# Normalisations and node scalings of a four-layer graph network: element work moved from VectorE to ScalarE, and one addition made by TensorE

## The chip, the cores and the metric

The kernel runs on one core of a Trainium2 chip. A core has five engines that run side by side, each with its own in-order queue of instructions: TensorE (PE in the profile; PEld is its loading of weights), VectorE (DVE), ScalarE (ACT), GpSimd (POOL) and SyncE (SP, which here only issues DMAs). They wait for one another through semaphores. The metric is device time in microseconds (us) from start to end of one execution; the median of three runs before the change is 2919.82 us.

## The reference

16 graphs (B) of 1024 nodes (N) with 64 features (H), each with a dense 1024 x 1024 fp32 adjacency. Four layers follow one another, and each begins with the same normalisation:

```
def _layernorm(x, axis=-1, eps=1e-5):
    m = jnp.mean(x, axis=axis, keepdims=True)
    v = jnp.var(x, axis=axis, keepdims=True)
    return (x - m) / jnp.sqrt(v + eps)
...
h = jnp.maximum(_layernorm(x, axis=-1), 0.0)
x = x + layer(h, adj)
```

- Layer 0: two small dense layers with relu, a product with the adjacency, and a gated (GRU) update.
- Layer 1: with `d = rowsum(adj + I) ** -0.5`, `relu(d_i * sum_j (adj + I)_ij * d_j * (h @ kernel)_j)`.
- Layer 2: part of the neighbours is struck off; per node and feature a weighted sum of three interpolated quantiles over the neighbours that are left (`agg`); then `relu((h + agg) @ W1 + b1) @ W2 + b2`, times the node mask.
- Layer 3: `(adj + I) @ h` divided by the row sums of `adj + I`.

## The kernel before

A tile holds the 1024 nodes of a graph as 128 partitions x 8 groups (`NT = 8`) x 64 features, so `X` and every feature tile of that kind is 128 x 512 fp32. A per-node number is a 128 x 8 tile; `over_h` broadcasts it over the 64 features.

The work on one graph is split into stages, each a Python generator: `load` (TensorE transposes the adjacency, ScalarE copies the result into `strip` and makes signs `sgn` of it), `code`, `rank`, `list` (which neighbours each node keeps, mostly VectorE), `mid` (`dense01`, lines 1277 to 1372: layers 0 and 1 and the normalisation of layer 2), `gath` (GpSimd fetches rows of neighbours' features, the table `tab`, with indirect DMAs), `sort` (VectorE sorts them with min/max networks; tiles `hb`, `s`, `o`), `sums` (ScalarE weights the sorted values, VectorE adds them), and `rear` (`dense23`, lines 1647 to 1699: rest of layer 2, and layer 3).

The order of all instructions is fixed before the program runs, by the planner `Order` (lines 191 to 273). It simulates the engines with costs from `Engine.duration` (326 to 356) and always takes a step of the stage that can start first; on a tie, the stage that is earlier in a list: `rear`, `sums` and `gath` come first, then `mid`, `list`, `rank` and `code`, then `load` and `fetch`, and `sort` last (1784). A generator's `yield "A", x` says that its next step is on ScalarE and needs `x`. The planner prices:

```
if self.letter == "V": ... return (cols + 74) / 960 + ..., 0.08
if self.letter == "A":
    return 0.09 + cols / 1130 + (0.2 if len(outs) > 1 else 0.0), 0.1
```

So changed steps change the order of everything around them. Stages of up to five graphs (`DEPTH = 5`) are under way at once. All instructions are issued by the helper at line 387, which is why the profile shows that line everywhere and tiles have to be told apart by name.

What the change touches: `layernorm_relu` (1181 to 1201), called three times in `dense01` (1281, 1344, 1370) and once in `dense23` (1683), 64 times over the 16 graphs; in `dense01` the product of the normalised `h` by `dinv` into `tr` (1353) and the update of X with `u1` (1362 to 1366); in `dense23` the addition of `agg` (gathered into `zz`) and `h2` with the transposition that follows (1661 to 1664), the product of the second dense layer's result by the node mask `nm` (1675 to 1679), and the division by the row sums (1688 to 1697). `transposed` (1206) and `back` (1216) are transpositions by TensorE; a `bank` is a PSUM buffer, given back by `close`. The tag `t2m` (and `t2r` in `dense23`) names two buffers that `t2` tiles share in turn; `hm` and `hr`, the normalised features, have one buffer each. In the profile tile names lose their trailing digits: `u1` and `u3` are `u`, `y2` is `y`.

The profile's line numbers are those of this listing.

Of the kernel before, what the change touches and what calls it, by code (L numbers as in the profile page):

```python
# [9 lines left out]
F32 = mybir.dt.float32  # L10
# [4 lines left out]
AF = mybir.ActivationFunctionType  # L15
ALU = mybir.AluOpType
AX = mybir.AxisListType

P = 128
# [373 lines left out]
def kernel(  # L393
# [29 lines left out]
    B, N, H = x.shape  # L423
    NT = N // P
    G = 3 * H
    HQ = q_W1.shape[1]
    NH = N // 512
# [4 lines left out]
    ident = const.tile([P, P], F32, name="ident")  # L432
# [75 lines left out]
    def over_h(v):  # L508
        return v[:, :, None].to_broadcast([P, NT, H])

    def lists_for_all():
        order = Order()
        V, A, T = Engine(nc.vector, "V", order), Engine(nc.scalar, "A", order), Engine(nc.tensor, "T", order)
# [10 lines left out]
        def bank(dtype=F32):  # L524
            return ps1.take([P, 512 * 4 // mybir.dt.size(dtype)], dtype, "bank")
# [42 lines left out]
        for k in range(8):  # L568
            v = NBITS * 2.0**k
# [608 lines left out]
                )  # L1178
                base += nr // 2 * q

        def layernorm_relu(X, h=None, who="m"):
            yield "V", X
            s = wp.tile([P, NT], F32, name="ln_s", bufs=2)
            V.reduce_sum(s, X, AX.X)
            V.tensor_scalar(s, s, -1.0 / H, None, ALU.mult)
            xc = wp.tile([P, NT, H], F32, name="ln_xc", tag="t2" + who, bufs=2)
            V.tensor_add(xc, X, over_h(s))
            sq = wp.tile([P, NT, H], F32, name="ln_sq", tag="t2" + who, bufs=2)
            yield "A", xc
            A.activation(sq, xc, AF.Square)  # L1190
            yield "V", sq
            v = wp.tile([P, NT], F32, name="ln_v", bufs=2)
            V.reduce_sum(v, sq, AX.X)
            yield "A", v
            A.activation(v, v, AF.Sqrt, bias=eps, scale=1.0 / H)
            yield "V", v
            V.reciprocal(v, v)
            if h is None:
                h = wp.tile([P, NT, H], F32, name="h" + who, bufs=1)
            V.scalar_tensor_tensor(h, xc, 0.0, over_h(v), ALU.max, ALU.mult)  # L1200
            return h

        def t2(name, who="m"):
            return wp.tile([P, NT, H], F32, name=name, tag="t2" + who, bufs=2)

        def transposed(h, dst):
            for i in range(NH):
                yield "T", h
                pt = yield from bank()
                for t in range(4):  # L1210
                    T.transpose(pt[0:H, t * P : (t + 1) * P], h[:, 4 * i + t, :], ident)
                yield "A", pt
                A.copy(dst[:, i * 512 : (i + 1) * 512], pt[0:H, :])
                ps1.close(pt)
# [62 lines left out]
        def dense01(b, S):  # L1277
            X = wp.tile([P, NT, H], F32, name="X", bufs=2)
            S_.dma_start(X, x[b].rearrange("(t p) h -> p t h", p=P))

            h = yield from layernorm_relu(X)
            cat = wp.tile([P, N], F32, name="cat")
            yield from transposed(h, cat[0:H, :])
            yield "T", cat
            m1T = wp.tile([P, N], F32, name="m1T", tag="big")
            pm = yield from product(w1, cat[0:H])
            yield from evicted(pm, m1T[0:H], AF.Relu, b1)
            yield "T", m1T
            p2 = yield from bank()
            T.matmul(p2, *bias(0), start=True, stop=False)  # L1290
            ams = streamed(b, 0)
            for t in range(NT):
                o = p2[:, t * H : (t + 1) * H]
                T.matmul(o, m1T[0:H, t * P : (t + 1) * P], w2, start=False, stop=t == NT - 1)
            yield "A", p2
            A.activation(m2x[:, :, 0:H], p2.rearrange("p (t h) -> p t h", h=H), AF.Relu)
            ps1.close(p2)
            pm = yield from propagated(b, m2x, 0, ams)

            yield "A", pm  # L1300
            A.copy(m1T[H : H + 1, :], pm[H : H + 1, :])
            yield from evicted(pm, cat[H:P], AF.Relu)
            yield "T", m1T
            pr = yield from bank()
            for t in range(NT):
                T.transpose(
                    pr[:, t : t + 1], m1T[H : H + 1, t * P : (t + 1) * P], ident[H : H + 1, H : H + 1]
                )
            yield "V", pr
            S["rs"] = rs = st.tile([P, NT], F32, name="rs")  # L1310
            V.tensor_scalar(rs, pr[:, 0:NT], 1.0, None, ALU.add)
            ps1.close(pr)
            rz = wp.tile([P, NT, 2 * H], F32, name="rz", tag="big")
            nn = t2("nn")
            for g in range(2):
                yield "T", cat
                pg = yield from bank2()
                for i in range(4):
                    t = 4 * g + i
                    o = pg[:, i * 4 * H : (i + 1) * 4 * H]  # L1320
                    if i % 2 == 0:
                        T.matmul(pg[:, i * 4 * H : (i + 2) * 4 * H], *bias(2), start=True, stop=False)
                    T.matmul(o, cat[:, t * P : (t + 1) * P], wg, start=False, stop=i % 2 == 1)
                pgv = pg.rearrange("p (i c) -> p i c", c=4 * H)
                gs = slice(4 * g, 4 * g + 4)
                yield "A", pg
                A.activation(rz[:, gs, :], pgv[:, :, 0 : 2 * H], AF.Sigmoid)
                yield "V", rz
                V.tensor_mul(nn[:, gs, :], pgv[:, :, 2 * H : G], rz[:, gs, 0:H])
                V.tensor_add(nn[:, gs, :], nn[:, gs, :], pgv[:, :, G : 4 * H])  # L1330
                ps2.close(pg)
            yield "A", nn
            A.activation(nn, nn, AF.Tanh)
            yield "V", nn

            d0 = t2("d0")
            V.tensor_sub(d0, h, nn)
            V.tensor_mul(d0, d0, rz[:, :, H : 2 * H])
            V.tensor_add(d0, d0, nn)
            V.tensor_add(X, X, d0)  # L1340

            ams = streamed(b, 1)

            h = yield from layernorm_relu(X)
            dinv = wp.tile([P, NT], F32, name="dinv", bufs=2)
            V.tensor_scalar(dinv, rs, 1e-30, None, ALU.max)
            yield "A", dinv
            A.activation(dinv, dinv, AF.Sqrt)
            yield "V", dinv
            V.reciprocal(dinv, dinv)  # L1350
            V.scalar_tensor_tensor(dinv, rs, 0.0, dinv, ALU.is_gt, ALU.mult)
            tr = t2("tr")
            V.tensor_mul(tr, h, over_h(dinv))
            pm = yield from propagated(b, tr, 1, ams, own=True)
            g0 = wp.tile([P, N], F32, name="g0", tag="big")
            yield from evicted(pm, g0[0:H])
            yield "T", g0
            pm = yield from product(wk, g0[0:H])
            g1 = wp.tile([P, N], F32, name="g1", tag="big")
            yield from evicted(pm, g1[0:H])  # L1360
            pa = yield from back(g1[0:H])
            yield "V", pa
            u1 = t2("u1")
            V.tensor_mul(u1, pa, over_h(dinv))
            ps1.close(pa)
            V.scalar_tensor_tensor(X, u1, 0.0, X, ALU.max, ALU.add)

            yield "S", X
            S_.dma_start(D[b % DEPTH]["x1"].rearrange("(t p) h -> p t h", p=P), X)
            h2 = yield from layernorm_relu(X)  # L1370
            yield "S", h2
            S_.dma_start(D[b % DEPTH]["tab"][1 : N + 1, :].rearrange("(t p) h -> p t h", p=P), h2)
# [274 lines left out]
        def dense23(b, S):  # L1647
# [7 lines left out]
            for t in range(NT):  # L1655
# [2 lines left out]
                    out=zz[:, t, :], out_offset=None, in_=d["agg"][:, :],  # L1658
                    in_offset=bass.IndirectOffsetOnAxis(ap=S["posi"][:, t : t + 1], axis=0),
                )  # L1660
            yield "V", zz
            V.tensor_add(zz, zz, h2)
            zT = wp.tile([P, N], F32, name="zT", tag="big3")
            yield from transposed(zz, zT[0:H])
            yield "T", zT
            uT = wp.tile([P, N], F32, name="uT", tag="big3")
            pm = yield from product(v1, zT[0:H])
# [4 lines left out]
            for t in range(NT):  # L1672
                o = py[:, t * H : (t + 1) * H]
                T.matmul(o, uT[:, t * P : (t + 1) * P], v2, start=False, stop=t == NT - 1)
            yield "V", py
            y2 = t2("y2", "r")
            V.tensor_mul(y2, py.rearrange("p (t h) -> p t h", h=H), over_h(nm))
            ps1.close(py)
            V.tensor_add(X, X, y2)

            ams = streamed(b, 3)
# [3 lines left out]
            g3 = wp.tile([P, N], F32, name="g3", tag="big3")  # L1685
            yield from evicted(pm, g3[0:H])
            pa = yield from back(g3[0:H])
            yield "V", pa
            u3 = t2("u3", "r")
            rd = wp.tile([P, NT], F32, name="rd", bufs=2)  # L1690

            V.scalar_tensor_tensor(rd, rs, 0.0, rs, ALU.is_equal, ALU.add)
            V.reciprocal(rd, rd)
            V.tensor_mul(u3, pa, over_h(rd))
            ps1.close(pa)
            res = t2("res", "r")
            V.tensor_add(res, X, u3)
            yield "S", res
# [472 lines left out]
```

## Time and profile before

| | |
|---|---|
| median of 3 runs (range) | 2919.82 us (2914.99 to 2942.51) |
| the profiled execution, its own time | 2917.36 us |
| its span (first to last instruction) | 2915.5 us, 31549 instructions |
| mean granted TensorE clock | 0.732 |
| VectorE busy, instructions | 2520.7 us (86%), 6678 |
| ScalarE busy, instructions | 1260.2 us (43%), 3138 |
| GpSimd busy, instructions | 1782.6 us (61%), 1598 |
| TensorE matmul busy | 1852.8 us (64%) |
| DMA | 427.11 MB, 146 GB/s over the span |

The page of the profile gives busy times, 40 equal slices with the busy share of each engine in tenths, and groups of instructions: engine, operation, output <- inputs, partitions x elements and type, times; then busy us, mean ns of one, and the engine's idle time just before them with what ended it. A row of the waits view reads: engine, tile, `<-` what it waited for, then us in total, times, longest. A row of the chain reads: start in us, duration, what ran. A share of busy time is a mean over stages with different limits; the stretches and the waits say which holds where.

### The profile page before, as it was taken

What the parts mean: (1) busy time and instruction counts of PE and PEld (TensorE: products, weight loads), DVE (VectorE), ACT (ScalarE), POOL (GpSimd) and SP (SyncE); (2) the same over time, 40 slices, a digit from 0 to 9 for tenths busy, and PEclk for the clock granted to TensorE, in tenths of its full rate; (3) what the DMA queues carried; (4) which work ended last, traced back from release to release, by engine and by line L of the source; (5) the groups of instructions that cost most, each with busy time, mean ns of one, the idle gap of its engine ahead of it and who ended that gap; (6) DMA issues with size and microseconds to landing.
All of it is one profiled execution on the core that took longest, in us unless ns stands there. A gap on an engine that the chain in (4) does not pass through costs nothing. (4 is left out here: it accounts for less than half of the span.)

```text
span 2915.5 us, 31549 instructions
## 1 busy us (share of the span) xinstructions
PE 1852.8 (64%) x8258; PEld 937.5 (32%) x8258; DVE 2520.7 (86%) x6678; ACT 1260.2 (43%) x3138; POOL 1782.6 (61%) x1598
## 2 busy tenths in 40 slices
PE   5876768677577776656856766767665865442223
PEld 3443333334233333233332433334232422121111
DVE  3659899988989979999798988899899799989792
ACT  7666373436445445335254355344445343030201
POOL 3047673746847567575656747566674667677761
PEclk6977779778787776877867667767876877656566
DMA  6667565465565546455564556536565643222222
GB/s 187 198 201 211 146 180 182 128 196 156 181 173 154 182 133 193 122 160 154 147 172 112 161 142 189 155 107 184 148 176 138 175 132 105 59 63 62 62 60 76
DMA packets 395166, 427.11 MB, mean 146 GB/s; under 512 B 165980, under 2 KB 302754, under 8 KB 394978
## 3 DMA queue, kind: packets, MB, share of 16 engines
q1 hardware_dynamic: 344386, 374.35, 41.9%
q0 software_dynamic: 50592, 50.66, 9.4%
q8 instruction: 68, 1.11, 0.2%
q14 instruction: 120, 0.98, 0.1%
HBM read 340.38 MB, written 84.46 MB: 146 GB/s over the span
## 5 line engine op out<-in xcount | busy, mean ns | idle before, releaser
L387 POOL DMA_INDIRECT s<-tab,idxL x864 | 1036.7, 1200 | 263.3 <-issue 259.1
L387 POOL DMA_INDIRECT gh<-tab,idxH x544 | 577.6, 1062 | 722.8 <-DVE idxH L387 169.6
L387 DVE TENSOR_TENSOR hb<-hb 128x128 f32<-128x128 f32 (+11 forms) x1072 | 739.1, 725 | 32.0 <-ACT hb L387 26.8
L387 PE MATMUL bank<-am,hr 128*64 128x512 f32 x512 | 281.9, 699 | 128.3 <-DVE hr L387 80.5
L387 PE MATMUL bank<-am,tr 128*64 128x512 f32 x512 | 270.4, 664 | 101.0 <-DVE tr L387 79.6
L387 PE MATMUL bank<-am,m2x 128*65 128x512 f32 x512 | 265.5, 662 | 45.1 <-DMA am<-adjT 40.5
L387 DVE TENSOR_TENSOR hb<-hb,hb 128x656 f32<-128x656 f32 (+2 forms) x256 | 252.3, 1000 | 3.9
L387 PE MATMUL bank<-ident,a 128*128 128x128 f32 x1024 | 202.3, 353 | 46.2 <-DMA a<-in_adj_dram 23.9
L387 ACT ACTIVATE s<-s,wl 128x64 f32<-128x64 f32 x704 | 180.3, 341 | 78.2 <-DVE s L387 78.2
L387 ACT COPY strip<-bank 128x512 f32<-128x512 f32 x256 | 143.5, 585 | 132.9 <-PE bank L387 121.1
L387 POOL DMA_INDIRECT zz<-agg,posi x128 | 141.4, 1104 | 87.4 <-DMA agg<-s 41.3
L387 PE MATMUL bank<-ident,gh 128*128 128x128 f32 x272 | 89.0, 352 | 154.1 <-DMA gh<-tab,idxH 153.3
L387 PEld LDWEIGHTS bank<-ident,a 128*128 128x128 f32 x1024 | 156.4, 183 | 77.5 <-issue 23.4
L387 PE MATMUL bank<-cx,oh 128*128 128x133 f16 (+1 forms) x1280 | 157.1, 279 | 35.5 <-DVE oh L387 25.4
L387 PEld LDWEIGHTS bank<-am,hr 128*64 128x64 f32 x512 | 74.6, 159 | 307.0 <-issue 137.1
L387 ACT ACTIVATE sgn<-strip 128x1024 bf16<-128x1024 f32 x128 | 135.2, 1056 | 53.0 <-PE bank L387 39.5
L387 ACT ACTIVATE junk<-bank,nkey 128x1024 bf16<-128x1024 f32 x128 | 140.7, 1108 | 27.5 <-PE bank L387 27.4
L387 PEld LDWEIGHTS bank<-am,tr 128*64 128x64 f32 x512 | 68.4, 150 | 237.6 <-issue 145.3
L387 ACT ACTIVATE g<-bank 64x512 f32<-64x512 f32 x96 | 52.0, 584 | 213.3 <-PE bank L387 213.3
L387 DVE TENSOR_TENSOR s<-s,o 128x576 f32<-128x576 f32 (+5 forms) x256 | 139.2, 552 | 2.8
L387 DVE TENSOR_TENSOR o<-s 128x1152 f32<-128x1152 f32 (+2 forms) x192 | 140.0, 754 | 1.6 <-DMA gh<-tab,idxH 0.2
L387 PE MATMUL bank<-w,sgn 128*128 128x32 bf16 x1024 | 49.8, 184 | 142.8 <-DVE sgn L387 97.2
(340 smaller groups left out, 3634.0 us busy)
## 6 DMA issues: line engine op xcount, KB each, us to landing
am<-adjT SPq DMA_DIRECT2D x384, 512.0 KB
a<-in_adj_dram SPq DMA_DIRECT2D x128, 512.0 KB
adjT<-strip SPq DMA_DIRECT2D x128, 512.0 KB
s<-tab,idxL POOLq DMA_INDIRECT x864
gh<-tab,idxH POOLq DMA_INDIRECT x544
wb<-wd SPq DMA_DIRECT2D x32, 198.0 KB
X<-in_x_dram SPq DMA_DIRECT2D x16, 256.0 KB
x<-X SPq DMA_DIRECT2D x16, 256.0 KB
```

The lines of the kernel that those rows point to most:

```text
L387: return f(*args, **kw)
```

## The change

- `layernorm_relu`: the centred copy `xc` and the tile of squares are gone. ScalarE takes the squares straight from X, one instruction for each of the 8 groups, with minus the mean as bias and the sum over the features from the instruction's accumulator; the squares themselves are written into the place of the result and overwritten later. VectorE multiplies minus the mean by the reciprocal deviation, and ScalarE makes `relu(X * v - mean * v)`, again 8 instructions. A new argument `times` multiplies the reciprocal deviation by a further per-node number.
- Layer 1's `tr` comes out of the normalisation so, with `times = dinv`; `dinv` is made ahead of it.
- A new helper `scaled` multiplies by a per-node number on ScalarE, 8 instructions; it takes the place of VectorE's product in `u1` (with the relu), `y2` and `u3`.
- The addition of `h2` to `zz` is made by TensorE: the transposition of `zz` becomes a product with the identity, and a second product adds `h2`.

```diff
-        def layernorm_relu(X, h=None, who="m"):
+        def layernorm_relu(X, h=None, who="m", times=None):
             yield "V", X
             s = wp.tile([P, NT], F32, name="ln_s", bufs=2)
             V.reduce_sum(s, X, AX.X)
             V.tensor_scalar(s, s, -1.0 / H, None, ALU.mult)
-            xc = wp.tile([P, NT, H], F32, name="ln_xc", tag="t2" + who, bufs=2)
-            V.tensor_add(xc, X, over_h(s))
-            sq = wp.tile([P, NT, H], F32, name="ln_sq", tag="t2" + who, bufs=2)
-            yield "A", xc
-            A.activation(sq, xc, AF.Square)
-            yield "V", sq
+            yield "A", s
             v = wp.tile([P, NT], F32, name="ln_v", bufs=2)
-            V.reduce_sum(v, sq, AX.X)
-            yield "A", v
+            if h is None:
+                h = wp.tile([P, NT, H], F32, name="h" + who, bufs=1)
+            for t in range(NT):
+                A.activation(h[:, t, :], X[:, t, :], AF.Square, bias=s[:, t : t + 1], accum_out=v[:, t : t + 1])
             A.activation(v, v, AF.Sqrt, bias=eps, scale=1.0 / H)
             yield "V", v
             V.reciprocal(v, v)
-            if h is None:
-                h = wp.tile([P, NT, H], F32, name="h" + who, bufs=1)
-            V.scalar_tensor_tensor(h, xc, 0.0, over_h(v), ALU.max, ALU.mult)
+            if times is not None:
+                V.tensor_mul(v, v, times)
+            V.tensor_mul(s, s, v)
+            yield "A", s, v
+            for t in range(NT):
+                A.activation(h[:, t, :], X[:, t, :], AF.Relu, bias=s[:, t : t + 1], scale=v[:, t : t + 1])
             return h
+
+        def scaled(dst, src, by, func=AF.Copy):
+            for t in range(NT):
+                A.activation(dst[:, t, :], src[:, t, :], func, scale=by[:, t : t + 1])
...
-            h = yield from layernorm_relu(X)
             dinv = wp.tile([P, NT], F32, name="dinv", bufs=2)
...
             V.scalar_tensor_tensor(dinv, rs, 0.0, dinv, ALU.is_gt, ALU.mult)
-            tr = t2("tr")
-            V.tensor_mul(tr, h, over_h(dinv))
+            tr = yield from layernorm_relu(X, t2("tr"), "m", dinv)
...
-            yield "V", pa
+            yield "A", pa
             u1 = t2("u1")
-            V.tensor_mul(u1, pa, over_h(dinv))
+            scaled(u1, pa, dinv, AF.Relu)
             ps1.close(pa)
-            V.scalar_tensor_tensor(X, u1, 0.0, X, ALU.max, ALU.add)
+            yield "V", u1
+            V.tensor_add(X, X, u1)
...
-            yield "V", zz
-            V.tensor_add(zz, zz, h2)
             zT = wp.tile([P, N], F32, name="zT", tag="big3")
-            yield from transposed(zz, zT[0:H])
+            for i in range(NH):
+                yield "T", zz, h2
+                pt = yield from bank()
+                for t in range(4):
+                    o = pt[0:H, t * P : (t + 1) * P]
+                    T.matmul(o, zz[:, 4 * i + t, :], ident, start=True, stop=False)
+                    T.matmul(o, h2[:, 4 * i + t, :], ident, start=False, stop=True)
+                yield "A", pt
+                A.copy(zT[0:H, i * 512 : (i + 1) * 512], pt[0:H, :])
+                ps1.close(pt)
...
-            yield "V", py
+            yield "A", py
             y2 = t2("y2", "r")
-            V.tensor_mul(y2, py.rearrange("p (t h) -> p t h", h=H), over_h(nm))
+            scaled(y2, py.rearrange("p (t h) -> p t h", h=H), nm)
             ps1.close(py)
+            yield "V", y2
             V.tensor_add(X, X, y2)
...
-            yield "V", pa
+            yield "V", rs
             u3 = t2("u3", "r")
             rd = wp.tile([P, NT], F32, name="rd", bufs=2)
             V.scalar_tensor_tensor(rd, rs, 0.0, rs, ALU.is_equal, ALU.add)
             V.reciprocal(rd, rd)
-            V.tensor_mul(u3, pa, over_h(rd))
+            yield "A", pa, rd
+            scaled(u3, pa, rd)
             ps1.close(pa)
+            yield "V", u3
             res = t2("res", "r")
             V.tensor_add(res, X, u3)
```

## The prediction, made before the changed kernel ran

> **What bounds the kernel now.** I read the page first (busy shares and the 40 slices), then the busy times in stretches of 100 us, the groups with their shapes kept apart, the waits, the chain that ended last, and single stretches of the timelines.
>
> ```profile
> PE 1852.8 (64%) x8258; PEld 937.5 (32%) x8258; DVE 2520.7 (86%) x6678; ACT 1260.2 (43%) x3138; POOL 1782.6 (61%) x1598
> ...
> DVE  3659899988989979999798988899899799989792
> ```
>
> VectorE (DVE) is the fullest engine (second line: tenths busy in 40 slices), and outside the fill (the first 200 us) and the tail (the last 65 us) it is at 79 to 97% in every stretch. ScalarE (ACT) is at 67 to 72% in the first 300 us, at 40 to 53% until 2400, then at 11 to 29%. From 200 to 2800 us VectorE stands idle for only 238 us of 2600 (the stretches of 100 us, summed), and what ends those gaps is spread thin:
>
> ```profile
> DVE oc L387 <- PE bank L387: 32.5, 11, 10.9
> DVE idxH L387 <- PE bank L387: 29.6, 10, 6.8
> DVE sgn L387 <- ACT sgn L387: 29.6, 13, 4.0
> DVE hb L387 <- ACT hb L387: 26.8, 7, 11.9
> ```
>
> These are its four longest (us in total, times, longest). Adding up this view over all rows, ScalarE ends 145 us of VectorE's waits and TensorE 138 us. So the bound is VectorE's own work plus small gaps; the sorting stages, which come last in the planner's order of stages, fill VectorE whenever nothing else is ready. The tail is different: there the chain is a latency chain through one graph. Its normalisation reads:
>
> ```profile
> 2882.31 0.70 DVE ln_s L387
> 2883.03 0.18 DVE ln_s L387
> 2883.24 0.70 DVE ln_xc L387
> 2883.96 0.64 ACT ln_sq L387
> 2884.62 0.70 DVE ln_v L387
> 2885.35 0.31 ACT ln_v L387
> 2885.68 0.21 DVE ln_v L387
> 2885.91 0.70 DVE hr L387
> ```
>
> From the first sum to `hr` ready: 4.3 us, of which VectorE is busy 3.2 us.
>
> **What the Trainium skill says.** "Perfetto Trace Analysis", section Identifying the Most-Contended Engine, takes the engine of highest occupancy as the one to relieve; here that is VectorE at 86%, so work taken from it should count. "VectorE: DVE Perf Modes", section on the TRN2 errata, gives an fp32 two-tensor operation (N+151)/0.96 ns, an estimate of 691 ns at N = 512; the trace has 692. "ScalarE: Activation LUTs", section What ACT_TABLE_LOAD costs, gives an ACTIVATE 186 ns + 0.833 ns per element, 93 ns more for each per-partition scale or bias, and 93 ns of overlap between neighbours. For 64 columns and one such operand that is an estimate of 239 ns from start to start; the trace has 15 of `s<-s,wl` (64 columns, a per-partition scale) in 3.69 us, so 0.246. Its section Rules for kernel authors sends relu and mul to VectorE; this change goes against that, and per operation it does lose (below).
>
> **The change part by part.** Rows, from the groups with shapes kept apart:
>
> ```profile
> L387 DVE TENSOR_REDUCE ln_v<-ln_sq 128x8 f32<-128x512 f32 x64 | 43.2, 675 | 4.5 <-ACT ln_sq L387 4.2 <-issue 0.2
> ...
> L387 DVE TENSOR_TENSOR ln_xc<-X,ln_s 128x512 f32<-128x512 f32 x48 | 33.4, 697 | 1.6
> ...
> L387 DVE SCALAR_TENSOR_TENSOR hm<-ln_xc,ln_v 128x512 f32<-128x512 f32 x48 | 33.3, 693 | 1.7
> ...
> L387 ACT ACTIVATE s<-s,wl 128x64 f32<-128x64 f32 x704 | 180.3, 341 | 78.2 <-DVE s L387 78.2
> ...
> L387 ACT ACTIVATION_READ_ACCUMULATOR junk<-bank,nkey 128x1 f32 x128 | 25.7, 201 | 0.0
> ```
>
> VectorE, removed. The first three rows with the `Xr` and `hr` forms of the last two (11.1 each) are 64 normalisations times three operations: 44.5 + 43.2 + 44.4 = 132 us. One large product or sum in each of five places a graph goes too: `tr` 11.1, `u<-bank,dinv` 10.9, `zz` 11.0, `y` 10.9, `u<-bank,rd` 11.1: 55 us. (The update of X with `u1` only changes its form.) Together 187. Added: a 128x8 product `s*v` in each normalisation and a product by `dinv` in 16 of them: 80 small operations at 0.19 (the reciprocal's row, 12.4/64): 15 us. Net 172. Neighbours on VectorE overlap: on its timeline a 0.69 us operation gives way to an independent one after 0.60 to 0.61, so 272 large operations may be worth 22 us less: 150. I take 160, and 15/16 of it, 150, as lying in the stretch that VectorE bounds; graph 0's normalisations lie in the fill, graph 15's last part in the tail.
>
> ScalarE, added. Squares: 8 a normalisation, each with a per-partition bias and an accumulator. No row has exactly that. The accumulator's read lasts 201 ns, but on the timeline a `junk` pair needs only 0.09 more than its ACTIVATE, as the read overlaps. Bounds: 0.25 (free) to 0.45 (read not overlapped); I take 0.246 + 0.09 = 0.34, so 2.7 us. Relus: 8 with scale and bias; one more operand is 0.09 by the skill's price, so 0.34 (0.25 to 0.43), 2.7 us. The old Square over 512 columns, 0.63, goes. +4.8 us in 64 normalisations = 306 us. The scalings `u1`, `y2`, `u3`: 48 times 8 times 0.246 = 94 us. ScalarE rises by 400 us to about 1660, 57% of the span (+310 at the lower, +500 at the upper prices). Table loads stay at 34: Square, Relu and Copy cause none now, and the order sigmoid, tanh, square root stays.
>
> TensorE. A transposition of `zz` (8 in 1.92 us in the tail) becomes 16 fp32 products with the identity; 8 such, `ident,hr`, take 1.91. So +1.9 us a graph, 30 in all, on an engine at 64%, hidden under VectorE's sort (30 us if TensorE were the bound).
>
> Buffers. `ln_xc` and `ln_sq` leave the two `t2` buffers, so those waits can only shrink. `hm` is written earlier, at the squares, and must wait for the previous graph's store to `tab`; that store is issued ahead of the next X load on the same SP queue, so I cost it nothing (if not covered: 2.6 us, the longest that a first sum waited for its X load, would be 42 over 16 graphs). No DMA is added or moved past another.
>
> Chains. A normalisation becomes 0.70 + 0.18 + 2.75 + 0.31 + 0.21 + 0.19 + 2.75 and hops, 7.2 us: 2.9 later than the 4.3 above. `tr` gains 0.69 back and loses a product: +2.4. `u1`, `y2`, `u3` take 2.0 for 0.70: +1.3 each. Fill (graph 0, before its first gather): 2.9 + 2.4 + 1.3 + 2.9 = 9.5. Tail: 2.9 + 1.3 + 1.3 + 1.9 (products) - 0.7 (no `zz` addition) = 6.7. Together 16 us. Elsewhere the chain is longer by the same 16 us a graph, hidden by the sort: X is loaded every 154 us (first 42.0, last 2349.8) and graph 0's middle stage took 107.
>
> New waits. ScalarE's queue is in order. Behind a block of 8 squares or relus stand the evictions of `strip`, `keys`, `cx` and `rz`, on which VectorE's `sgn`, `keys` and `nn` steps wait. I let the 145 us that ScalarE ends grow with its load, 400/1260 = 32%: 47 us, and the 138 of TensorE, which waits for banks to be emptied, by a tenth: 14. The planner prices a 64-column ACTIVATE at 0.09 + 64/1130 = 0.15 us against 0.25 here, so it sets VectorE's three additions up to 0.8 us too early: 38 us if all of it is felt, I take a third, 12. Sum 73, bounds 0 and about 230.
>
> Sum: 2915.5 - 150 + 16 + 73 = 2854 us of span. The profiled execution lies 2.4 us under the median of the runs and 1.9 over its span, so a median of about **2859 us**, 2.1% less.
>
> **Rivals.**
> (a) ScalarE's queue becomes the pace-setter, slower than before. For it: half of VectorE's gaps already end in ScalarE, it is at 70% in the fill, and it loses on every operation moved: 5.4 us for the 0.63 + 2.06 that it replaces. Against: at 57% it has 1250 us to spare, and its own idle is mostly waiting for VectorE and TensorE. It decides from where the gaps grow by 134 us (283 by 47%); at a growth of two thirds, 190, the span is 2915 - 150 + 16 + 190 = 2971.
> (b) Another engine takes over, and about half of the gain goes. GpSimd's gathers are 1782.6 busy and 424 of issue (259.1 + 124.0 + 40.7), 2206 in all, and from 2600 to 2800 us it shows 79% busy, which with 0.3 of issue per gather is full. If the gathers of the last two graphs set the end, what VectorE saves there is lost: 2915 - 75 + 16 + 40 = 2896, no change. Against: in the waits view VectorE waits 24 us for gathers, 14 of them in the tail.
> (c) Nearly no new waits, as the planner orders around them: 2915 - 150 + 16 = 2781. This is the forecast's mechanism with its smallest price.
>
> **How the numbers follow.** Forecast, gaps growing by 30 to 120 us (2811 to 2901): 0.48. (c): 0.14. (b): 0.16. (a): 0.22. About 1% is what a measurement of this kernel can tell from no change; that is 2891 and 2949. Of the forecast 0.45 is below 2891 and, with (c) and a little of (b), faster is 0.63. (a) from 2949 on gives slower 0.19; the rest, 0.18, is the same. The range reaches from (c) with the higher removal (172 for 160: 2770) to the beginning of (a), 2960.
>
> **What would show it.** Right: `ln_xc` and `ln_sq` gone; VectorE near 2350 to 2370 busy, ScalarE near 1660; 512 accumulator reads more; squares 0.34 and relus 0.34 from start to start; VectorE's waits on ScalarE near 200. Wrong: VectorE below 82% busy in the middle stretches, with waits on `h`, `keys`, `nn`, `u` or `sgn` grown past 280; or the same 90% with GpSimd at 79% throughout.

## The result and the profile after

| | before | after |
|---|---|---|
| median (18 runs each, range) | 2923.79 us (2905.54 to 2942.51) | 2900.41 us (2889.62 to 2910.99) |
| ratio, 95% interval | | 0.992 (0.990 to 0.994) |
| profiled execution, its span | 2917.36, 2915.5 | 2900.52, 2898.7 |
| VectorE busy, idle | 2520.7, 395 | 2367.7, 531 |
| ScalarE busy, instructions | 1260.2, 3138 | 1642.2, 4996 |
| GpSimd busy | 1782.6 | 1789.1 |

0.8% less, where the forecast was 2.1%. The interval excludes 1, so there is a gain, but not the one that was forecast. The page, busy times and VectorE's 40 slices:

```profile
PE 1893.6 (65%) x8642; PEld 973.4 (34%) x8642; DVE 2367.7 (82%) x6486; ACT 1642.2 (57%) x4996; POOL 1789.1 (62%) x1598
...
DVE  2458898898987989777897989989897789999691
```

VectorE did lose the forecast work (153 us), and ScalarE took up 382. But VectorE's idle time grew by 136, and 153 - 136 is the 17 us by which the span fell. The first slices are emptier (2458 for 3659) and the middle has sevens and eights where it had nines.

The groups with shapes kept apart, for the first and third normalisation of the middle stage and for one scaling:

```profile
L387 ACT ACTIVATE hm<-X,ln_s,ln_v 128x64 f32<-128x64 f32 x256 | 88.1, 430 | 7.2 <-DVE ln_s L387 7.1
L387 ACT ACTIVATE hm<-X,ln_s 128x64 f32<-128x64 f32 x256 | 85.4, 341 | 51.5 <-DVE ln_s L387 42.4 <-DVE LF L387 6.9 <-DVE y L387 1.8
...
L387 ACT ACTIVATION_READ_ACCUMULATOR hm<-X,ln_s 128x1 f32 x256 | 49.5, 194 | 0.0
...
L387 ACT ACTIVATE y<-bank,nm 128x64 f32<-128x64 f32 x128 | 27.9, 331 | 23.4 <-PE bank L387 23.3
```

Busy time over count is what one instruction costs in its block of eight: relus 88.1/256 = 0.344 us and scalings 27.9/128 = 0.218. The eight squares with their eight reads of the accumulator take 2.77 us in the chain below, 0.346 a pair, though a read lasts 194 ns by itself: most of it overlaps. On the timeline, from start to start within a block, a relu or a square with its read takes 0.33 us and a scaling 0.20.

VectorE's longest waits:

```profile
DVE sgn L387 <- ACT sgn L387: 53.9, 27, 11.5
DVE Xr L387 <- ACT y L387: 49.3, 4, 24.7
DVE oh L387 <- PE bank L387: 39.7, 6, 13.3
DVE posi L387 <- ACT junk L387: 38.1, 9, 11.5
DVE res L387 <- ACT u L387: 25.1, 7, 21.8
DVE ln_v L387 <- ACT ln_v L387: 24.2, 13, 5.8
DVE idxH L387 <- PE bank L387: 21.6, 8, 8.0
```

Over all rows of this view ScalarE now ends 316 us of them (145 before), TensorE 117 (146; the forecast's 138 leaves out the wait of the final flags, 8.6), DMAs 25 (38). Part of that is only a new name. The end of the last graph was `u <- PE bank` with 20.0 us at the longest; it is `res <- ACT u` with 21.8, the same chain with ScalarE in between. `Xr <- ACT y` (49.3) likewise stands where VectorE waited 22.2 us for the gathered `zz`. New in substance are `sgn` (29.6 to 53.9), `posi` (6.1 to 38.1), `ln_v` (7.1 to 24.2), all behind ScalarE's queue, and `oh` (3.9 to 39.7), behind TensorE.

The normalisation in the chain that ended last:

```profile
2857.17 0.70 DVE ln_s L387
...
2858.09 2.77 ACT hr L387 x16
...
2861.66 0.45 ACT hr L387
...
2862.15 5.27 PE bank L387 x8
```

From the first sum to TensorE's start: 2862.15 - 2857.17 = 4.98 us, against 4.3 to `hr` before. TensorE begins once the first of the eight relus is done; the rest run beside it.

**Where the time went.** The starts of a few instructions in the trace cut the span into three: up to the last graph's list (`idxH` of graph 15, on VectorE), from there to the first gather of graph 15 (GpSimd), and the rest.

| kernel | `idxH` of graph 14 | of graph 15 | first gather of graph 15 | from there to the end |
|---|---|---|---|---|
| before | 2553.4 | 2677.9 | 2693.3 (15 later) | 222.2 |
| after | 2533.6 | 2625.0 | 2670.9 (46 later) | 227.8 |

VectorE finished its last list 52.9 us earlier. Then the gathers of graph 15 waited 30.6 us longer than before, and the tail took 5.6 more: -52.9 + 30.6 + 5.6 = -16.7. What they waited for is on GpSimd's timeline (start, us, operation, in brackets its idle time and what ended it). Before:

```profile
2691.92 1.04 POOL L387 DMA_INDIRECT s<-tab,idxL  x1 [0.30 <-issue]
2693.27 1.05 POOL L387 DMA_INDIRECT gh<-tab,idxH  x1 [0.30 <-DVE wl L387]
```

After:

```profile
2667.64 1.12 POOL L387 DMA_INDIRECT s<-tab,idxL  x1 [0.30 <-DMA s<-tab,idxL]
2669.07 1.53 POOL L387 DMA_INDIRECT s<-tab,idxL  x1 [0.30 <-issue]
2670.90 0.96 POOL L387 DMA_INDIRECT gh<-tab,idxH  x1 [0.30 <-issue]
```

In both, graph 14's last `s` gather runs right up to graph 15's first `gh`, with only the usual 0.30 of issue between. Graph 14's gathers take 137 us from end to end (2534.0 to 2670.9; 139 before), and graph 15's list now came only 91 us after graph 14's. So in both kernels the end hangs on graph 14's list, which came only 19.8 us earlier: -19.8 for the list, -2.6 for its gathers, +5.6 for the tail. VectorE up to that list (the stretch, its length, then VectorE's busy us and instructions, the granted TensorE clock, DMA share, GB/s), before:

```profile
0.00:2553.40 2553.40, 2241.37 (x6053) 0.75 0.55 158
```

After:

```profile
0.00:2533.60 2533.60, 2103.66 (x5891) 0.75 0.56 159
```

It had 137.7 us less to do, but stood idle for 429.9 us instead of 312.0, which is 117.9 more. Between the two lists it did 84 us of work where it did 115 before, and after the last one 180 for 165: part of why the last list came early is that other work was put behind it.

### The profile page after: what moved, and what is told of

It is laid out like the page before. It is cut to its first block, busy times and chain, and to the rows that moved or that the text cites. A ratio compares the mean times of both kernels' runs of the same rounds, so it can differ in the third digit from the quotient of the medians.

```text
span 2898.7 us, 34020 instructions
## 1 busy us (share of the span) xinstructions
PE 1893.6 (65%) x8642; PEld 973.4 (34%) x8642; DVE 2367.7 (82%) x6486; ACT 1642.2 (57%) x4996; POOL 1789.1 (62%) x1598
## 5 line engine op out<-in xcount | busy, mean ns | idle before, releaser
L387 POOL DMA_INDIRECT s<-tab,idxL x864 | 1025.1, 1186 | 263.3 <-issue 260.3
L387 POOL DMA_INDIRECT gh<-tab,idxH x544 | 588.3, 1081 | 682.3 <-DVE nz L387 255.6
L387 PE MATMUL bank<-am,hr 128*64 128x512 f32 x512 | 273.8, 679 | 114.4 <-ACT hr L387 56.6
L387 PE MATMUL bank<-am,tr 128*64 128x512 f32 x512 | 278.3, 686 | 63.7 <-ACT tr L387 43.8
L387 POOL DMA_INDIRECT zz<-agg,posi x128 | 148.8, 1163 | 100.1 <-DMA agg<-s 46.8
L387 PEld LDWEIGHTS bank<-ident,a 128*128 128x128 f32 x1024 | 149.2, 176 | 122.8 <-issue 34.9
L387 PEld LDWEIGHTS bank<-am,hr 128*64 128x64 f32 x512 | 71.7, 154 | 286.2 <-issue 155.9
L387 ACT ACTIVATE sgn<-strip 128x1024 bf16<-128x1024 f32 x128 | 135.4, 1058 | 27.9 <-PE bank L387 18.1
L387 ACT ACTIVATE sgn<-sgn 128x1024 bf16<-128x1024 bf16 x128 | 135.3, 1057 | 4.1
```

What stands on the lines that cost most here:

```text
L387: return f(*args, **kw)
```

## The experiments

The instruction order is the planner's, so every edit here also draws a new order; several runs therefore measure what an order alone is worth. Each ratio is to the kernel before, run beside it.

**ScalarE's new work left out.** The eight squares become one Square of the 128 x 8 means, the eight relus and each eight scalings one instruction over 512 columns without their factors. This kernel leaves the normalisation and the scalings uncomputed.

```diff
-            for t in range(NT):
-                A.activation(h[:, t, :], X[:, t, :], AF.Square, bias=..., accum_out=...)
+            A.activation(v, s, AF.Square)
...
-            for t in range(NT):
-                A.activation(h[:, t, :], X[:, t, :], AF.Relu, bias=..., scale=...)
+            A.activation(h, X, AF.Relu)
...
-            for t in range(NT):
-                A.activation(dst[:, t, :], src[:, t, :], func, scale=by[:, t : t + 1])
+            A.activation(dst, src, func)
```

> The changed kernel with ScalarE's new work left out: the eight squares become one tiny Square of the 128x8 mean, the eight relus one Relu over 512 columns without scale and bias, each scaling one ACTIVATE over 512 columns without its factor. So normalisation and node scalings are not computed; VectorE's instructions are those of the changed kernel. Theory A (ScalarE's longer queue holds up VectorE and the list stage): VectorE's waits on ScalarE fall from 316 us back to near the 145 of before and the time to 2780-2830 us. Theory B (the serial list stage sets the pace through its own waits behind sort operations, whatever ScalarE does): within 15 us of the changed kernel, 2885-2900.

2777.92 us, 0.951 (0.948 to 0.955). Its page:

```profile
PE 1858.5 (67%) x8642; PEld 959.6 (35%) x8642; DVE 2354.7 (85%) x6486; ACT 1292.4 (47%) x3250; POOL 1807.2 (65%) x1598
```

With VectorE as busy as in the changed kernel (2354.7 against 2367.7) and ScalarE near its old load, 122 us go. So VectorE's relief is worth about 5% by itself, and ScalarE's 350 us of extra work take back 122 us of it in the given order, and about 80 against the neutral orders below. (Its order is a further one, which is in either number.) The time is the one that theory A named, its sign isn't: ScalarE still ends 248 us of VectorE's waits, where the theory had them fall back to near 145.

**Three edits of the plan.** Eight more serial steps in each list; sorting stages that ask the planner after every instruction instead of two; right prices for ScalarE's 64-column instructions.

```diff
+            for _ in range(8):
+                V.tensor_scalar(half_i, half_i, 0, None, ALU.logical_shift_right)
+                yield ("V",)
```

> The changed kernel with eight idle shifts by 0 of a 128x2 tile added as eight more serial steps of VectorE to the list stage of each graph, about 0.1-0.16 us of VectorE each, 13-20 us in all. If VectorE's total work sets the pace: +13 to +20 us, 2913-2920. If the serial chain of list stages sets it (each step also waits for the sort operations ahead of it in the queue, 1-2.4 us a pair): +8 to +16 us a graph over 14 graphs, +100 to +220 us, 3000-3120.

2875.48 us, 0.982 (0.979 to 0.986): more serial work, and yet 25 us less than the changed kernel. Neither theory had that; it was the first sign that the order itself mattered.

```diff
                     V.tensor_tensor(plain(ol, p), plain(lo, p), mirror(hi, p), ALU.min)
+                    yield ("V",)
                     V.tensor_tensor(plain(oh, p), mirror(lo, p), plain(hi, p), ALU.max)
...
                     V.tensor_tensor(ol, lo, hi, ALU.min)
+                    yield ("V",)
                     V.tensor_tensor(oh, lo, hi, ALU.max)
...
-        def network(plan, view, each=2):
+        def network(plan, view, each=1):
```

> The changed kernel with the sort stage giving the planner a turn after every operation in place of every pair. VectorE's work is the same. If the list stage's steps wait behind pairs of sort operations and that sets the pace, the list stage gets shorter by up to 20-30 us a graph and the time falls, 2780-2870, until the gathers bound it. If VectorE's total work or ScalarE sets the pace: unchanged within 15 us, 2885-2915.

2791.11 us, 0.955 (0.951 to 0.958), with the waits ended by ScalarE at 278 us.

```diff
-            return 0.09 + cols / 1130 + (0.2 if len(outs) > 1 else 0.0), 0.1
+            few = cols == 64
+            return 0.09 + cols / 1130 + (0.1 * (len(ins) - 1) if few else 0.0) + ((0.1 if few else 0.2) if len(outs) > 1 else 0.0), 0.1
```

> The changed kernel with the planner's price of 64-column ScalarE operations set to what the trace shows (0.25 us with one per-node operand, 0.35 with two, 0.35 with one and an accumulator, in place of 0.15, 0.15 and 0.35). If VectorE's new waits come from steps that the planner puts too early, VectorE's waits on ScalarE fall from 316 by 50 or more and the time by 20-60, to 2840-2880. If they come from ScalarE's queue itself: within 15 us of 2900.

2828.95 us, 0.967 (0.963 to 0.970). The time fell, but not by what was thought: the waits ended by ScalarE did not fall (334 us for 316), those ended by TensorE did, to 60.

**Neutral orders.** One price of the planner is changed by 1 ns (VectorE, `cols + 75`) or 3 ns (ScalarE, 0.093), too little to mean anything but enough to draw another order, for both kernels.

> The kernel before with the planner's price of every VectorE operation raised by one column (1 ns): no instruction is added or removed, only the order that the planner writes changes. If orders are worth little: within 10 us of 2922. If the written order alone is worth a per cent or more: anywhere from 2850 to 2990.

2913.53 us, 0.997 (0.995 to 0.999).

> The kernel before with the planner's fixed price of a ScalarE operation raised by 3 ns: the order alone changes. Within 10 us of 2922 if orders are worth little; 2850 to 2990 if the order alone is worth a per cent or more.

2921.97 us, 0.999 (0.998 to 1.001).

> The changed kernel with the price of every VectorE operation raised by one column (1 ns): the order alone changes. Within 10 us of 2900 if the measured gain of 0.8% belongs to the change itself. If 2900 was one draw among orders: 2820 to 2890, nearer to the forecast of 2859.

2858.23 us, 0.977 (0.973 to 0.981).

> The changed kernel with the fixed price of a ScalarE operation raised by 3 ns: the order alone changes. Within 10 us of 2900 if the measured gain belongs to the change itself; 2820 to 2890 if 2900 was one draw among orders.

2863.03 us, 0.979 (0.971 to 0.987). In these two draws the old kernel hardly depends on the order (0.3% at most), while the changed one gains 37 and 42 us, though from two runs each.

**The changed kernel again, its two parts, and a control.**

> The changed kernel once more, unaltered, so that the kernels of this job and of the jobs before it can be set against it on one chip. Theory (the order drawn by the planner makes the difference between 2900 and the 2858 and 2863 us of the two nearly equal prices): 2900 us within 10, ratio 0.992, clock 0.734, VectorE's waits ended by TensorE near 115 us. Rival (that difference came from the chip or the hour, since the granted clock was 0.75 to 0.76 in all those runs): 2860 us within 15 and a clock near 0.755 here too.

2904.17 us, 0.993 (0.990 to 0.996), 122 us of waits ended by TensorE: the order makes the difference, not chip or hour. The granted TensorE clock goes with the order: 0.728 to 0.744 in the 25 runs of the given one, 0.744 to 0.759 in the neutral ones. Within those 25 runs the time falls by 5 us for 0.01 of clock, in 61 runs of the kernel before by 8 (weak trends), so the 0.017 between the means makes an estimate of 8 to 14 us out of some 40. No run set the clock apart from the order, and ten runs of one neutral order of the old kernel fall by 20 for 0.01, so a larger part isn't excluded.

The parts are the normalisations alone, with `tr`, and the rest of the diff alone (`u1`, `y2`, `u3`, `zz`).

> The kernel before with the normalisation part alone (squares and relus on ScalarE, layer 1's product by dinv inside); scalings and the addition to zz as before. Forecast's own terms: VectorE -128 net, counted -112; longer chains +11; new waits 306/400 of 73 = +56: 2921 - 45 = 2876 us, ratio 0.985, and the larger part of the loss of cover in the fill (list of graph 1 starting near 190 us). Theory (the parts work by their size, the order of a kernel scatters by some 20 us): 2855 to 2900. Rival (the two parts hinder each other in the given kernel, and the squares alone give the whole relief): 2840 or less.

2895.97 us, 0.991 (0.987 to 0.994).

> The kernel before with the other part alone: u1, y2 and u3 scaled by ScalarE, h2 added to zz by TensorE; normalisation as before. Forecast's own terms: VectorE -44 net, counted -38; chains +5; waits +17: 2905 us, ratio 0.9945; the TensorE additions are hidden. Theory (parts work by their size, scatter of the order 20 us): 2885 to 2925. Rival (this part is what hurts, by ScalarE reading PSUM banks longer, so that TensorE waits for banks): 2935 or more, with VectorE's waits ended by TensorE above 170.

2876.86 us, 0.983 (0.980 to 0.987). The large part lies within its theory's bounds but 20 us above its forecast of 2876, the small one 28 below its 2905, outside the bounds; neither rival came. The two gains add up to 27.6 + 46.7 = 74 us, more than the whole change gives in any neutral order. Each was seen in one order only, so how the gain divides between them stays open. The list of graph 1 begins at 199.9 us with the normalisations and at 158.9 with the rest: the late start belongs to the normalisations. In both kernels graph 15's gathers begin 0.5 us after its list, so a small gain like the 28 us of the normalisations can come without a late hand-over to GpSimd.

> The kernel before with the planner asked again after every single sort instruction instead of after two. Control for the same edit on the changed kernel, which took it from 2900 to 2791 us (-3.8%). Theory (finer turns help because the changed kernel has more ScalarE-ended gaps to fill, which the old one lacks): 2880 to 2920, little gain. Rival (finer turns of the sort help either kernel alike, and say nothing of the change): 2810, -3.8%.

2849.37 us, 0.974 (0.971 to 0.977). Finer turns help the old kernel too, by 2.6%, between what the two theories said. Between the two kernels with finer turns lie 58 us, 2.0%, although graph 15's gathers begin 66 us after their list in the old one and 49 in the changed one. A hand-over that GpSimd takes late does not by itself eat the gain.

**Whether the given order is an exception.**

> The changed kernel with VectorE's planner price 1 ns lower an instruction (cols + 73 for cols + 74), for a further order of the same instructions. Theory (the given order is an unfavourable draw; typical ones take 2.0% less than before): 2865 us within 15, VectorE's waits ended by TensorE 50 to 80 us. Rival (the two orders at 2858 and 2863 were lucky, 2900 is typical): 2890 to 2915, with TensorE-ended waits near 115.

2853.33 us, 0.977 (0.973 to 0.982) against the kernel before in its given order: a third neutral order far below 2900. TensorE ends 74 us of its waits.

> The kernel before with the planner's ScalarE prices put right for instructions of 64 columns (0.10 more for each pointer operand, accumulator 0.1), the control for the same edit on the changed kernel, which took 2829 us. The kernel before has 704 such instructions in the weighting of sorted values. Theory (the right price helps either kernel a little, the change itself is worth 2%): 2887 us within 15. Rival A (the old kernel gains nothing from it): 2920, so the change with right prices would be worth 3.1%. Rival B (the change is worth 0.7%): 2850.

2930.2 us, 1.005 (1.003 to 1.007). Rival A: the old kernel gains nothing by right prices, the changed one 71 us of 2900.

```diff
             for t in range(NT):
+                yield ("A",)
                 A.activation(h[:, t, :], X[:, t, :], AF.Square, ...)
...
             for t in range(NT):
+                yield ("A",)
                 A.activation(h[:, t, :], X[:, t, :], AF.Relu, ...)
```

> The changed kernel with its squares and relus handed to the planner one at a time instead of in blocks of eight, so that an eviction for another stage that is ready can be put between them; the work is the same. Theory (part of what ScalarE costs is the block of 2.7 us in front of evictions on which VectorE waits): VectorE's waits ended by ScalarE fall from 316 to 270 or less, 2830 us within 20, at the price of a longer normalisation chain that the sort hides. Rival (the waits come from ScalarE's total load and from the longer chains of the stages, not from the block): ScalarE-ended waits stay at 310 to 345 and the time lies with the other orders, 2855 to 2905.

2882.7 us, 0.989 (0.985 to 0.993). Of its waits view:

```profile
DVE sgn L387 <- ACT sgn L387: 53.7, 24, 7.4
```

`sgn` stands where it stood (53.9), and ScalarE ends 309 us in all. These are the rival's numbers, within a microsecond or so: in this order the block of eight is not what costs.

> The changed kernel with both edits that helped: the planner asked after every sort instruction, and ScalarE's 64-column prices put right. Theory (they act on different gaps: finer turns fill gaps with sort work, right prices stop additions being placed too early): 2765 us within 15, ScalarE-ended waits 250. Rival (finer turns have taken already what right prices gave; what is left is order scatter): 2790 within 15, waits near 278 as with the finer turns alone.

2808.37 us, 0.963 (0.959 to 0.967): no sum of the two gains, above even the rival's 2805, although ScalarE ends only 257 us of the waits. Finer turns alone are better.

Beside the last two kernels everything took a quarter longer, the kernel before 3647 us, with a granted clock of 0.67 to 0.71 (0.72 to 0.77 elsewhere). Only ratios and early starts are read from them.

> The kernel before with VectorE's planner price 1 ns lower, the partner of the changed kernel that took 2853 us so. Theory (the change is worth about 2% in equally planned pairs, the old kernel hardly depends on the order): 2915 us within 8, so the pair differs by 2.1%. Rival (this price suits both kernels): 2875, a pair difference of 0.7%.

3587.5 us, 0.983 (0.974 to 0.992). As a ratio this is the rival's figure (2875 of the usual 2919 is 0.985), and the theory's (0.999) lies outside the interval. Whether it holds at the usual speed is open, so the third pair stays without a partner of its own. But it speaks against a rule: set against the 0.977 of the changed kernel, this pair would differ by only 0.6%.

```diff
+            normal = layernorm_relu if b else layernorm_was
```

> The changed kernel in its order with VectorE's price 1 ns higher (2858 us), with graph 0's three normalisations of the middle stage in their old form; the other 61 are as changed. Theory (the start is paid for in full, because list stages run back to back from there on): the list stage of graph 1 starts near 160 instead of 194 us, and the end comes 25 to 35 us earlier, 2828 us within 8. Rival A (forecast: only the longer chains of graph 0 count, 8 us of the 9.5, the rest is made up later): 2850 within 6. Rival B (nothing of it reaches the end, orders scatter by 10): 2858 within 8 with list 1 at 160.

3427.74 us, 0.938 (0.926 to 0.950); it can't be set against 2858. The list of graph 1 began at 156.1 us, so graph 0's own normalisations cause the late start, and not those of graph 1. Whether that reaches the end stays open.

**The pairs together**, changed over before in the same plan (ratios of the ratios above, so without an interval of their own; the pair with VectorE's price - 1 ns is left out, as its two sides ran at different speeds):

| plan | before | changed | ratio |
|---|---|---|---|
| given | 2923.79 | 2900.41 | 0.992 |
| VectorE's price + 1 ns | 2913.53 | 2858.23 | 0.980 |
| ScalarE's price + 3 ns | 2921.97 | 2863.03 | 0.980 |
| turn after every sort instruction | 2849.37 | 2791.11 | 0.980 |
| right 64-column prices | 2930.2 | 2828.95 | 0.962 |

Three of the five lie at 2.0%, the others at 0.8 and 3.8%. And the three stretches of the span for the neutral orders:

| kernel | `idxH` of graph 14 | of graph 15 | first gather of graph 15 | from there to the end |
|---|---|---|---|---|
| VectorE + 1 ns, before | 2537.1 | 2685.1 | 2685.6 | 235.3 |
| VectorE + 1 ns, changed | 2480.5 | 2630.5 | 2631.0 | 222.2 |
| ScalarE + 3 ns, before | 2540.0 | 2690.0 | 2690.4 | 230.8 |
| ScalarE + 3 ns, changed | 2490.8 | 2640.0 | 2640.4 | 229.6 |
| VectorE - 1 ns, changed | 2481.7 | 2633.4 | 2633.9 | 225.7 |
| changed kernel again | 2533.7 | 2627.6 | 2676.0 | 226.6 |

GpSimd's timeline of the changed kernel with VectorE's price + 1 ns, at the same place as above:

```profile
2618.43 1.00 POOL L387 DMA_INDIRECT s<-tab,idxL  x1 [0.31 <-issue]
2630.99 1.04 POOL L387 DMA_INDIRECT gh<-tab,idxH  x1 [11.55 <-DVE idxH L387]
```

Here graph 14's gathers end at 2619.4, GpSimd stands idle 11.55 us, and VectorE's `idxH` releases the next ones. The last list comes at 2625 to 2640 in all five runs of the changed kernel, earliest in the given order. But there graph 14's list comes 43 to 53 us later than in the neutral orders, and its gathers are in the way of graph 15's. That is read from the traces; no run moved graph 14's list alone. VectorE up to graph 14's list with VectorE's price + 1 ns, in the same columns as above, before:

```profile
0.00:2537.10 2537.10, 2241.41 (x6047) 0.75 0.57 159
```

Changed:

```profile
0.00:2480.50 2480.50, 2095.40 (x5864) 0.78 0.58 163
```

VectorE's work up to there is nearly the same in the two orders of the changed kernel, 2103.7 us in the given one and 2095.4 in this one, so graph 14's list is late because VectorE stands idle: for 429.9 us in the given order, 385.1 in this one. Of its waits up to that list TensorE ends 116 us in the given order (114 before) and 52, 66 and 53 in the neutral ones; ScalarE ends 238 for 257, 250 and 266. So what the given order lacks is the fall of the waits for TensorE. Over the whole span the wait for `oh` alone is 39.7 for 0.5 to 15.5. `oh` has one buffer for all graphs, written again when TensorE is done with the graph before; no run gave it a second one, so what makes the list late there stays open.

The start is alike in all orders of the changed kernel. The stretches now have all engines (busy us and instructions of TensorE, its weight loads, VectorE, ScalarE, GpSimd), here before, then the given order, then VectorE's price + 1 ns changed:

```profile
0.00:200.00 200.00, 140.56 (x862) 88.25 (x863) 99.52 (x480) 138.94 (x277) 48.41 (x85) 0.75 0.70 206
...
0.00:200.00 200.00, 129.38 (x664) 74.44 (x665) 79.64 (x411) 135.00 (x328) 44.76 (x80) 0.72 0.58 170
...
0.00:200.00 200.00, 130.84 (x668) 75.44 (x669) 80.54 (x416) 135.00 (x328) 45.45 (x81) 0.85 0.58 172
```

## Why the prediction was right or wrong

- **VectorE's work: right.** 150 to 172 us were to go, taken as 160; busy time fell by 153.
- **ScalarE's prices: right.** +382 us for +400. Squares and relus cost the forecast 0.34; for the relus that was the trace's 0.246 plus the 93 ns that the Trainium skill's "ScalarE: Activation LUTs", section What ACT_TABLE_LOAD costs, gives for one more operand. Scalings from PSUM were cheaper, 0.218. Table loads are 36, not 34.
- **TensorE: too small, and right in the tail by luck.** It runs 384 matmul instructions more, 24 a graph, and is busy for 41 us more, for 30. In the tail the products of `zz` and `h2` last 5.6 us (2844.27 to 2849.87) where the transpositions lasted 1.9: 3.7 more, for 1.9. The forecast's sum still comes out, because the four products after them took 1.9 us at a granted clock of 1.00, and before the change 3.7 at 0.50.
- **Chains: near in the fill, wrong in the tail's parts.** Graph 0's first gather starts 11.1 us later (159.8 to 170.9) for 9.5, but not through the longer middle stage (its table is stored at 155.9 for 155.1): the list got later (`half_i` of graph 0 at 79.8 for 72.3, of graph 1 at 195.0 for 158.4). That graph 0's normalisations cause the second delay is shown by the run with their old form (156.1); that it is by standing ahead of the list on ScalarE is argued. In the tail the stretch from the last block of weighting to `res` got shorter, 58.4 to 55.6 us. The relus overlap with TensorE, so the normalisation is 0.6 us longer and not 2.9; above all TensorE starts on `zz` 7.6 us after `agg` is stored, for 13.0: at 2844.3, before the last gather of `zz` goes out at 2846.2, while the addition on VectorE waited for all of them. Afterwards came 6.7 us that the forecast did not have: the flags' last sums, done before within the tail (2879), now follow `res` at 2886, because their PSUM bank was the last one that `u3` was read from. That is a draw of the order too: what follows `res` takes 12.7 us in the given order, 5.9, 12.9 and 6.8 in the neutral ones, and in the old kernel 6.0, 12.8 and 7.1.
- **New waits: too small in the given order, and wrong in the parts.** 73 us were forecast, 59 on ScalarE and 14 on TensorE. With the 9.5 of the fill and the 10 of graph 0's work that the forecast did not count as gain, VectorE was to stand idle for some 92 us more. Up to graph 14's list it was 118 in the given order; in the pairs with VectorE's price + 1 ns and ScalarE's + 3 ns it was 89 and 103. By name ScalarE's waits grew by 172 in the given order and TensorE's fell by 29, partly one turned into the other; in the two pairs they grew by 205 and 204 and fell by 85 and 75. Waits on ScalarE near 200 were named as a sign of being right, past 280 as one of being wrong: they are 316, and 336 to 344 in the faster neutral orders, so this sign tells nothing. Of the places named `sgn` was right, `keys` grew little (13.6 to 19.4) and `nn` not (22.6 to 19.8); `posi`, behind the ranks' eight sign instructions, was not thought of. The mispriced additions, put at 12 with 38 as their bound, may be worth 24 to 34 (2829 against the neutral 2853 to 2863); that is one order, and not one with fewer waits on ScalarE.
- **The end: the step that failed.** The sum let every us that VectorE saves up to its last list reach the end, and put nothing for the hand-over to GpSimd. Rival (b) said where it would not: "If the gathers of the last two graphs set the end, what VectorE saves there is lost", worked out as 2896. It was set aside because VectorE waits little for gathers. That was the wrong row: a finished list that lies waiting leaves no wait on VectorE, and before the change graph 15's gathers already began 15 us after their list, straight behind graph 14's. In the given order that became 45.9. Of the 44 us between the forecast 61 and the measured 17, this hand-over is 31; another 14 are missing at the last list (52.9 us earlier for 67), and the tail is 1 better than forecast.

Told by graph 14's list instead, from which GpSimd's work runs through, the same miss is VectorE's idle time: the list came only 19.8 us earlier, where it came 57 and 49 earlier in the two pairs. So the late hand-over and the waits that did not fall are two sides of one order. Which of them would have to go for the 31 us to come back is not shown, as no run moved graph 14's list alone.

The Trainium skill's "Perfetto Trace Analysis", section Optimization Strategy, says that the most-contended engine can change from one regime of a kernel to the next. Busy shares alone do not show it in this trace. In the stretch of graph 14's gathers in the changed kernel VectorE, which fills in sorting, is busy for 129 of 137 us and GpSimd for 107. Only with the 0.30 of issue before each of its 96 DMAs is GpSimd full there.

```profile
2534.00:2670.60 136.60, 45.18 (x236) 23.89 (x236) 128.84 (x346) 37.70 (x146) 107.06 (x96) 0.64 0.28 66
```

So both mechanisms are there. In the neutral orders, where graph 14's list comes early enough, the forecast's 2859 is what is measured (2853 to 2863), partly by luck, since the waits on ScalarE were put far too low and those on TensorE fell instead of growing. In the given order the late hand-over of rival (b) takes 31 us; why that order keeps VectorE waiting for TensorE is open. Rival (a) did not come: ScalarE's load costs 80 to 122 us but stays under the relief. The kernel with finer turns of the sort, 2791 us, beats both.

## What to carry to other kernels

Before a saving on the fullest engine is counted to the end, follow the last units of work from engine to engine and ask at each hand-over which side is late: here the list was done 15 us before GpSimd could take it, in a profile where no large wait said so. When a planner writes the order, a change is one draw; two or three neutral changes of a price, before and after, show how much of a result is the order. Here equally planned pairs gave 0.8 to 3.8%, three of five 2.0%.

## What the runs showed of the hardware

- Each engine ran its instructions in one order: in two profiled executions of the changed kernel (the result and the one run again) ScalarE's 4996 and VectorE's 6486 came in the same sequence.
- The accumulator's read lasts 194 ns, but a block of eight squares with their reads takes 2.77 us, 0.346 a pair, as much as a relu without a read and with one more operand (0.344).
- A 64-column scaling with one operand cost 0.218 us when it read PSUM (`y`, `u`), and 0.246 in the weighting `s<-s,wl`, which reads SBUF.
- Four products with `zT` took 3.7 us at a granted clock of 0.50 and 1.9 at 1.00.
- The granted clock of TensorE in the first 200 us was 0.72 in the changed kernel and 0.85 in the one with VectorE's price + 1 ns, at nearly the same work, and the list of graph 1 began at 195.0 and 194.0: between these two runs the start did not hang on TensorE's clock.
